# Moving a third of a causal convolution into the stage ahead of it

## The chip, the cores and the metric

The kernel runs on one core of a Trainium2 chip. The metric is the device time of one execution in microseconds (us); the median of 3 runs of the kernel before is 3901.01 us (3900.33 to 3903.65). The engines named below are PE (matrix multiply), DVE (elementwise, the vector engine), ACT (activations, the scalar engine), POOL (elementwise on small things, and one of the queues that issue transfers) and SP (only issues transfers). [...]

## The reference

Two layers on x of shape (4, 512, 128, 64): 4 batches, T = 512 steps, D = 128 x 64 = 8192 columns. The first layer is, for each batch:

```
xn = layernorm(x);  k, v, r = xn @ Wk, xn @ Wv, sigmoid(xn @ Wr)
s_t = decay * s_(t-1) + k_t * v_t            # scan over time
x = x + (r * s) @ Wo
x = x + gelu(conv3 over f of layernorm(x))   # per time step, 64 x 64 channels
xn = layernorm(x)
to = depthwise causal conv over time of xn, 3 taps, + time_b
x = x + layernorm(to) * g + b                # over the 8192 columns of a step
x = x + gelu(x @ W1 + b1) @ W2 + b2          # on the 64 channels
```

The second layer takes a moving average over 25 steps, multiplies the low 128 frequencies of the rest by complex weights, and adds the two. The change touches the first layer only, and there the line `to = ...` and the sums over columns that the layernorm after it needs.

## The kernel before

**Tiling.** In layer 1 the 8192 columns lie on the partitions in 64 chunks of 128, and the 512 time steps lie along the free dimension, so a shift in time is a shift of the free index. Most code handles a pair of chunks at once, a tile of 128 x 2 x 512 (512 KB); a batch has 32 pairs (NPR). Moments over the columns are sums over partitions, and PE makes them by matmuls with a tile of ones.

**Stages of a batch.** J (`project`) makes k, v, r and the statistics of x. Z (`scan`) is the recurrence. A (`attend_and_convolve`) adds the attention, makes the convolution over f, writes the result to DRAM as x2d and sums it. C (`convolve_time`) is the causal convolution: it loads x2d, applies the layernorm with rows rb and mb (one multiply, one subtract), makes three taps, writes the result to DRAM as tod, squares it and sums both. O (`open_feed`) and F (`feed_forward`) load tod and x2d again, make the residual x3 and run the feed-forward, chunk by chunk: `widen` (two matmul groups and two gelus), `narrow` (into the one-bank PSUM tile pa, read by DVE into x4t), `store` (a transpose through PSUM, a copy, a store).

**Order.** The stages are Python generators, and `in_turn` runs two lanes of them against each other: Z, A of batch 0 beside J of 1; C(0) beside A(1); F(0) beside J(2) and Z(2); C(1) beside A(2); F(1) beside J(3) and Z(3); C(2) beside A(3); F(2) beside C(3); F(3) alone. A number in brackets is the batch. `tc.manual_schedule` fixes this written order for PE alone. The orders of DVE, ACT, POOL and of the transfer queues are made by a planner, which places an instruction where its own reckoning finds the engine free, and may draw it far ahead of its place in the source.

**The work of C on one pair** (lines 570 to 586): DVE has the multiply (L570), the subtract into a padded tile xh (L572) and four taps (L579: two for each of the two chunks, each multiplying a shifted view of xh and adding it to `to`); ACT makes the last tap with the bias first (L575) and the squares at the end (L585); POOL zeroes the two columns of padding (L571), adds a correction to the first two time steps (L583) and issues the store (L584); SP issues the load (L547 within `fetch`). PE sums `to` and its squares two pairs later (`add_up`, L249).

**The work of A on one pair**: DVE has three tensor operations of 1024 columns (L482 x1, L486 z, L518 x2). **Of F on two chunks**: DVE has three for the residual (L597, L598, L609) and two x4t (L645); beside it J has two scalings of weights (L355) and two statistics (L342) per pair. J's matmuls are L358; `widen` is L629, `narrow` is L640, the gelus are L633, the transposes L654.

**Buffers.** Tiles with the same tag share a few buffers. C of batches 0 to 2 uses kx (3), kd (2), kh (2, for xh), k3 (3); A uses x1 (3) and z (4), which no stage uses while F stands beside J. The rows rb and mb of C are in the tile rm3, as are those of Z.

Of the kernel before, what the change touches and what calls it, by code (L numbers as in the profile page):

```python
# [10 lines left out]
F32 = mybir.dt.float32  # L11
AF = mybir.ActivationFunctionType
ALU = mybir.AluOpType
# [3 lines left out]
P = 128  # L17
# [5 lines left out]
SL = 512  # L23
NS = D // SL
NPR = NCH // 2
NT = T // P
S = 64
# [14 lines left out]
G1, B1, G2, B2, G3, B3, TB, G4, B4, W0, W1, W2 = range(12)  # L42
# [37 lines left out]
def layer0(ctx, tc, dram, x, xt, vecs, wkvr, wo, wdec, wconv, fbias, w1, fb1, w2, fb2, x4):  # L80
# [4 lines left out]
    nc = tc.nc  # L85
    B = x.shape[0]

    x2d = [dram.tile([NCH, P, T], F32, tag=f"x2_{b}", name=f"x2_{b}") for b in range(B)]
    tod = [dram.tile([NCH, P, T], F32, tag=f"to_{b}", name=f"to_{b}") for b in range(B)]
# [4 lines left out]
    bk = ctx.enter_context(tc.tile_pool(name="bk", bufs=2))  # L94
# [8 lines left out]
    def two(pool, tag):  # L103
        return pool.tile([P, 2, SL], F32, tag=tag, name=tag)
# [16 lines left out]
    def load(name, src):  # L121
        t = const.tile(list(src.shape), F32, name=name)
        nc.scalar.dma_start(t, src)
        return t

    vec = load("vec", vecs)
# [26 lines left out]
    tb_all = const.tile([P, NCH], F32, name="tb_all")  # L153
    fix = const.tile([P, NCH, 2], F32, name="fix")

    halves = [slice(0, H), slice(H, P)]

    def neighbours(q, c):
# [85 lines left out]
    def add_up(st, i, pair, squares, first, last):  # L244

        for j in range(2):
            for k, src in ((0, pair), (1, squares)):
                q = 2 * j + k
                nc.tensor.matmul(  # L249
                    st[32 * q : 32 * q + 32, :], lhsT=ones, rhs=src[:, j, :],  # L250
                    start=first, stop=last,
                )
# [25 lines left out]
    def rows(bank, a, b, names):  # L278
        both = rowp.tile([P, 2, SL], F32, tag=names, name=names)
        for k, col in enumerate((a, b)):  # L280
            pb = bank()
            spread(pb, col)
            nc.scalar.copy(both[:, k, :], pb)
            yield CHAIN
        return both[:, 0, :], both[:, 1, :]

    def pair_of(row):
        return row.unsqueeze(1).to_broadcast([P, 2, SL])
# [6 lines left out]
    def spare(tag, n):  # L295
        return fr.tile([P, 2, n], F32, tag=tag, name=tag, bufs={"z": 4, "wx": 2}.get(tag, 3))

    def c_bank():
        return two(ps_c, "c")
# [9 lines left out]
    carried = {}  # L309
    causal = {}  # L310
    scale = {}
    opened = {}
    begin = {}
    free_s = [True]
    held = [False]
# [53 lines left out]
    def scan(b):  # L369
        kvrg, stt, *left = projected.pop(b)  # L370
        bank = of_p if b == 1 else of_a
        rs, sq = cols("rs1"), cols("sq1")
        mean = cols("mean1")
# [35 lines left out]
            nc.vector.tensor_copy(qo[S:P, 0:S], pq[S:P, 0:S])  # L409
            nc.vector.tensor_scalar_mul(qo[S:P, S:], pq[S:P, S + 2 :], 1.0 / D)  # L410
        gw, bw, qo = sums["gw"], sums["bw"], sums["qo"]
        rb, mb = yield from rows(bank, rs, mean, "rm3")
        if b == 0:
            kv = two(fr, "x1")
        else:
# [42 lines left out]
        rs, mrs = moments(mean2, sq, 2)  # L458
# [84 lines left out]
        carried[b] = moments(mean3, sq3, 3)  # L543

    def fetch(tag, src, b, i):
        t = bk.tile([P, 2, SL + 2], F32, tag=tag, name=tag, bufs=3 if tag == "kx" else 2)[:, :, 0:SL]
        nc.sync.dma_start(t, src[b][2 * i : 2 * i + 2].rearrange("c p t -> p c t"))  # L547
        return t


    def convolve_time(b):
        bank = of_a if b == B - 1 else of_p
        rb, mb = yield from rows(bank, *carried.pop(b), "rm" if b == B - 1 else "rm3")
        st = bank()
        waiting = {}
        for i in range(NPR + 2):
            if i > 1:
                add_up(st, i - 2, *waiting.pop(i - 2), i == 2, i == NPR + 1)
            if i < NPR:
                if b == B - 1:  # L560

                    x2, xr, to = spare("xp", SL), spare("x1", SL), spare("z", SL)
                    xh = spare("wx", 4 * S + SL)[:, :, 0 : SL + 2]
                    sq = two(bk, "sq")
                    nc.sync.dma_start(x2, x2d[b][2 * i : 2 * i + 2].rearrange("c p t -> p c t"))
                else:
                    x2, xr, to = fetch("kx", x2d, b, i), two(bk, "kd"), bk.tile([P, 2, SL], F32, tag="k3", name="to", bufs=3)
                    xh = bk.tile([P, 2, SL + 2], F32, tag="kh", name="xh")
                    sq = bk.tile([P, 2, SL], F32, tag="sq4", name="sq4", bufs=2)
                nc.vector.tensor_tensor(xr, x2, pair_of(rb), ALU.mult)  # L570
                nc.gpsimd.memset(xh[:, :, 0:2], 0.0)  # L571
                nc.vector.tensor_tensor(xh[:, :, 2:], xr, pair_of(mb), ALU.subtract)  # L572
                for j in range(2):
                    c = slice(2 * i + j, 2 * i + j + 1)
                    nc.scalar.activation(  # L575
                        to[:, j, :], xh[:, j, 2:], AF.Identity, bias=tb_all[:, c], scale=vec[:, W2, c]
                    )
                    for k, w in ((1, W1), (0, W0)):
                        nc.vector.scalar_tensor_tensor(  # L579
                            to[:, j, :], xh[:, j, k : SL + k], vec[:, w, c], to[:, j, :], ALU.mult, ALU.add  # L580
                        )
                cc = slice(2 * i, 2 * i + 2)
                nc.gpsimd.tensor_tensor(to[:, :, 0:2], to[:, :, 0:2], fix[:, cc, :], ALU.add)  # L583
                nc.gpsimd.dma_start(tod[b][cc].rearrange("c p t -> p c t"), to)  # L584
                nc.scalar.activation(sq, to, AF.Square)  # L585
                waiting[i] = to, sq
            yield 7.0
        mean, sq = yield from finish(st, bank, 4)
        causal[b] = moments(mean, sq, 4)

# [29 lines left out]
    def feed_forward(b):  # L620
        x3s = opened.pop(b)
        mids, x4s, obs = {}, {}, {}

        def widen(c, m):
            x3 = x3s[c // 2][:, c % 2, :]
            pm = c_bank() if m else two(ps_m, "m")
            for h in range(2):
                hs = slice(h * H, (h + 1) * H)
                nc.tensor.matmul(  # L629
                    pm[:, h, :], lhsT=w1_sb[hs, m * P : (m + 1) * P], rhs=x3[hs, :], start=True, stop=True  # L630
                )
            mid = mids[c, m] = bk.tile([P, 2, SL], F32, tag="mid", name="mid", bufs=4)
            nc.scalar.activation(mid, pm, AF.Gelu_apprx_tanh, bias=fb1_sb[:, m : m + 1])  # L633

        def narrow(c):
            pa = ps_p.tile([P, SL], F32, tag="p", name="pa")
            for m in range(2):
                mid = mids.pop((c, m))
                for h in range(2):
                    nc.tensor.matmul(  # L640
                        pa[h * H : (h + 1) * H, :], lhsT=w2_sb[:, m, :], rhs=mid[:, h, :],
                        start=(m == 0), stop=(m == 1),
                    )
            x4t = x4s[c] = bk.tile([P, SL], F32, tag="x4t", name="x4t", bufs=3)
            nc.vector.scalar_tensor_tensor(x4t, pa, fb2_sb, x3s[c // 2][:, c % 2, :], ALU.add, ALU.add)  # L645
            if c % 2:
                x3s.pop(c // 2)

        def store(c):
            x4t = x4s.pop(c)  # L650
            pool, tag = (ps_s, "s") if free_s[0] else (ps_p, "p")
            pt = pool.tile([P, NT, P], F32, tag=tag, name="pt")
            for t in range(NT):
                nc.tensor.transpose(pt[:, t, :], x4t[:, t * P : (t + 1) * P], ident)  # L654
            s = c // 4
            if c % 4 == 0:
                obs[s] = bk.tile([P, NT, SL], F32, tag="ob", name="ob")
            o = obs[s][:, :, c % 4 * P : (c % 4 + 1) * P]
            if c // 2 % 2:
                for h in range(2):  # L660
                    nc.scalar.copy(o[:, :, halves[1 - h]], pt[:, :, halves[h]])  # L661
            else:
                nc.scalar.copy(o, pt)
            if c % 4 == 3:
                nc.gpsimd.dma_start(  # L665
                    x4[b][:, s * SL : (s + 1) * SL].rearrange("(t p) d -> p t d", p=P), obs.pop(s)
                )

        for c in range(NCH + 2):
            if c < NCH:  # L670
                widen(c, 0)
                widen(c, 1)
            i = c // 2 + 2
            if i < NPR:
                if c % 2:
                    x3s[i] = add_residual(b, i, *coming)
                else:
                    coming = residual(b, i)
            if 0 < c <= NCH:
                narrow(c - 1)  # L680
            if c > 1:
                store(c - 2)
            yield 4.5
# [360 lines left out]
```

## Time and profile before

| | us |
|---|---|
| median of 3 runs | 3901.01 |
| the profiled execution | 3909.18 |
| its span (first to last instruction) | 3907.4 |
| PE busy | 3679.3 (94%) |
| DVE busy | 2686.3 (69%) |
| ACT busy | 1726.6 (44%) |
| POOL busy | 582.5 (15%) |
| transfers, mean over the span | 231 GB/s |
| L579, the taps of C: 384 instructions | 277.0, 745 ns each |
| L640, `narrow`: idle before it, waiting for DVE's x4t | 48.0 |

Busy time is a share of the whole span, and the stages have different limits, so the shares above say little about a single stage. A line of the groups view names the source line, the engine, the operation, what it writes and reads, the size and the count; then its busy time and the mean of one in ns; then how long the engine stood idle just before such instructions, and what ended that. Matmuls overlap one another, so PE's busy time is the time in which at least one was running. In the stages of the first layer, C(0) beside A(1) lies at about 530 to 820 us of the span, F(0) beside J(2) at 850 to 1237, C(1) beside A(2) at 1240 to 1525, F(1) beside J(3) at 1557 to 1940, C(2) beside A(3) at 1945 to 2230, and F(2) beside C(3) up to about 2510.

### The profile page before, as it was taken

The numbers are of one execution on the slowest core, as the hardware profiler recorded it, in microseconds if no ns is written. First come the engines' busy times: TensorE is split into PE (matmuls) and PEld (weight loads), VectorE is DVE, ScalarE is ACT, GpSimd is POOL, SyncE is SP. The second block draws the span as 40 slices with busy tenths as digits, with TensorE's granted clock in tenths as the row PEclk, the third lists the DMA queues.
The fourth block names the chain that finished last, engine by engine and source line by source line (L and its number), as shares of the span: only waits on it lengthen the run. The fifth ranks groups of instructions, "written<-read, shape, count | busy, mean of one in ns | idle before, by whom it ended". The sixth has DMA issues, their size and how long they took to land. (4 is left out here: it accounts for less than half of the span.)

```text
span 3907.4 us, 44936 instructions
## 1 busy us (share of the span) xinstructions
PE 3679.3 (94%) x15945; PEld 1344.5 (34%) x15945; DVE 2686.3 (69%) x3498; ACT 1726.6 (44%) x2427; POOL 582.5 (15%) x1038
## 2 busy tenths in 40 slices
PE   9999998899999898999998888999989999999999
PEld 4433322233333222333322222333322753326533
DVE  4445659975555997555599899955558267892587
ACT  0023345555555564555655588867742210022100
POOL 0000012210000222000022221100014100151011
PEclk9999999999999999999999999999999999999999
DMA  9857647776663777666477677645558468994587
GB/s 310 267 202 250 220 152 250 255 252 237 231 231 142 248 262 253 220 236 235 155 240 244 243 252 256 227 149 185 182 182 286 153 208 295 312 302 149 193 295 268
DMA packets 426166, 901.27 MB, mean 231 GB/s; under 512 B 35864, under 2 KB 86232, under 8 KB 421848
## 3 DMA queue, kind: packets, MB, share of 16 engines
q1 hardware_dynamic: 343552, 621.97, 48.1%
q0 software_dynamic: 79872, 274.77, 19.5%
q8 instruction: 127, 2.08, 0.2%
q10 hardware_dynamic: 2520, 1.67, 0.1%
q14 instruction: 95, 0.78, 0.1%
HBM read 629.77 MB, written 268.50 MB: 230 GB/s over the span
## 5 line engine op out<-in xcount | busy, mean ns | idle before, releaser
L640 PE MATMUL pa<-mid,w_sb 128*64 128x512 f32 x2048 | 498.1, 607 | 48.0 <-DVE x4t L645 48.0
L633 ACT ACTIVATE mid<-m,fb_sb 128x1024 f32<-128x1024 f32 x256 | 284.9, 1113 | 291.1 <-PE m L629 290.7
L645 DVE SCALAR_TENSOR_TENSOR x4t<-pa,fb_sb,x 128x512 f32<-128x512 f32 x252 | 188.0, 746 | 241.2 <-PE pa L640 241.1
L629 PE MATMUL m<-x,w_sb 64*128 64x512 f32 x1008 | 288.3, 644 | 1.5 <-ACT mid L633 0.8
L579 DVE SCALAR_TENSOR_TENSOR to<-xh,vec,to 128x512 f32<-128x512 f32 x384 | 277.0, 745 | 10.7 <-issue 6.8
L633 ACT ACTIVATE mid<-c,fb_sb 128x1024 f32<-128x1024 f32 x256 | 283.3, 1107 | 1.2 <-PE c L629 1.2
L629 PE MATMUL c<-x,w_sb 64*128 64x512 f32 x1008 | 262.7, 594 | 1.3 <-ACT mid L633 1.3
L640 PEld LDWEIGHTS pa<-mid,w_sb 128*64 128x64 f32 x2048 | 124.9, 136 | 391.5 <-issue 229.5
L358 PE MATMUL a<-xp,wx 128*128 128x512 f32 x512 | 241.0, 597 | 6.4 <-DVE wx L355 5.9
L249 PE MATMUL st<-x,ones 128*32 128x512 f32 x512 | 206.4, 616 | 34.3 <-DVE x L518 34.2
L912 PE MATMUL b<-xin,avg_sb 128*128 128x512 f32 x512 | 230.8, 593 | 3.3 <-DVE xin L918 3.3
L918 DVE TENSOR_TENSOR xin<-b,pm 128x512 f32<-128x512 f32 x256 | 159.0, 683 | 97.7 <-PE b L915 82.7
L889 ACT COPY two<-a 128x512 f32<-128x512 f32 x64 | 37.5, 585 | 426.7 <-PE a L884 426.7
L355 DVE TENSOR_SCALAR wx<-wx,vec 128x192 f32<-128x192 f32 x174 | 48.3, 317 | 241.2 <-DMA wx<-in_wkvr 217.4
L665 POOL DMA_DIRECT2D x<-ob x64 | 49.0, 766 | 1049.8 <-ACT ob L661 980.6
L606 ACT ACTIVATE kd<-kd,vec 128x512 f32<-128x512 f32 x256 | 193.6, 809 | 4.3 <-DVE kd L598 4.3
L521 ACT ACTIVATE sq<-x 128x1024 f32<-128x1024 f32 x128 | 134.6, 1051 | 134.7 <-DVE x L518 134.4
L815 DVE TENSOR_TENSOR uv<-xin 128x1024 f32<-128x1024 f32 x128 | 155.8, 1224 | 50.7 <-PE a L829 33.5
L480 PE MATMUL a<-rst,wo_sb 64*128 64x512 f32 x512 | 153.3, 673 | 34.4 <-DVE x L482 33.3
L585 ACT ACTIVATE sq<-to 128x1024 f32<-128x1024 f32 x96 | 101.3, 1055 | 188.7 <-POOL xh L571 183.1
L575 ACT ACTIVATE to<-xh,tb_all,vec 128x512 f32<-128x512 f32 x192 | 149.4, 803 | 77.4 <-DVE xh L572 64.0
L794 DVE COPY xf<-b 128x256 f32<-128x256 f32 x128 | 54.4, 425 | 183.4 <-PE b L858 182.8
(236 smaller groups left out, 6768.2 us busy)
## 6 DMA issues: line engine op xcount, KB each, us to landing
xp<-in_xt SPq DMA_DIRECT2D x256, 512.0 KB
xin<-x SPq DMA_DIRECT2D x128, 1024.0 KB
kx<-x SPq DMA_DIRECT2D x224, 512.0 KB
x<-x POOLq DMA_DIRECT2D x128, 512.0 KB, 4.6
kh<-to SPq DMA_DIRECT2D x128, 512.0 KB
x<-ob POOLq DMA_DIRECT2D x64, 1024.0 KB, 6.6
out<-xin POOLq DMA_DIRECT2D x64, 1024.0 KB, 6.9
to<-to POOLq DMA_DIRECT2D x96, 512.0 KB, 4.2
```

What stands on the lines that cost most here:

```text
L249: nc.tensor.matmul(st[32 * q : 32 * q + 32, :], lhsT=ones, rhs=src[:, j, :], start=first, stop=last,)
L358: nc.tensor.matmul(pa[:, k, :], lhsT=wq[:, j, k * P : (k + 1) * P], rhs=xp[:, j, :], start=first and j == 0, stop=last and j == 1,)
L480: nc.tensor.matmul(at[:, j, :], lhsT=wo_sb[js, :], rhs=rst[js, :], start=True, stop=True)
L579: nc.vector.scalar_tensor_tensor(to[:, j, :], xh[:, j, k : SL + k], vec[:, w, c], to[:, j, :], ALU.mult, ALU.add)
L606: tc.keep_in_program_order(nc.scalar.activation(d[:, j, :], d[:, j, :], AF.Identity, bias=vec[:, B4, c], scale=vec[:, G4, c]))
L629: nc.tensor.matmul(pm[:, h, :], lhsT=w1_sb[hs, m * P : (m + 1) * P], rhs=x3[hs, :], start=True, stop=True)
L633: nc.scalar.activation(mid, pm, AF.Gelu_apprx_tanh, bias=fb1_sb[:, m : m + 1])
L640: nc.tensor.matmul(pa[h * H : (h + 1) * H, :], lhsT=w2_sb[:, m, :], rhs=mid[:, h, :], start=(m == 0), stop=(m == 1),)
L645: nc.vector.scalar_tensor_tensor(x4t, pa, fb2_sb, x3s[c // 2][:, c % 2, :], ALU.add, ALU.add)
L815: nc.vector.tensor_tensor(t, xin[:, 0:2, :], xin[:, 2:4, :], op)
L912: nc.tensor.matmul(po[j], lhsT=avg_sb[:, j, :], rhs=xin[:, j, :], start=True, stop=False)
L918: nc.vector.tensor_tensor(by_n(xin[:, j, :]), by_n(po[j]), by_c(pm[j % 2][:, j // 2, :]), ALU.add)
```

## The change

Twelve of the 32 pairs of the causal convolution of batches 1 and 2 are made one stage earlier, in F(0) and F(1). A generator `convolve_ahead` makes the rows rb and mb in rm3 in its first two steps, and one pair in each of the next twelve; `feed_forward` takes a step of it at every fourth chunk (c = 3, 7, ... 63, of which the first fourteen have something to do). Such a pair is loaded into x1, normalized in place there, made into a tile z and stored to tod. It is not summed then: `convolve_time` of that batch makes the other 20 pairs and, spread among them, loads the twelve back from tod (into kh), squares them on ACT and sums both, so that the sums over all 32 pairs are made in C as before. The rows are taken over from the stage ahead.

The function `taps` holds what both places do. In it the padded tile xh is gone for all batches: the normalized tile stays in xr, and the taps on earlier steps write the shorter views `to[:, j, 1:]` and `to[:, j, 2:]`, so POOL's zeroing is gone as well. The scans of batches 2 and 3 put their rows into rm, since rm3 stays in use from F to C.

```diff
-        rb, mb = yield from rows(bank, rs, mean, "rm3")
+        rb, mb = yield from rows(bank, rs, mean, "rm" if b > 1 else "rm3")
...
+    def taps(b, i, x2, xr, to, rb, mb):
+
+        nc.sync.dma_start(x2, x2d[b][2 * i : 2 * i + 2].rearrange("c p t -> p c t"))
+        nc.vector.tensor_tensor(xr, x2, pair_of(rb), ALU.mult)
+        nc.vector.tensor_tensor(xr, xr, pair_of(mb), ALU.subtract)
+        for j in range(2):
+            c = slice(2 * i + j, 2 * i + j + 1)
+            nc.scalar.activation(
+                to[:, j, :], xr[:, j, :], AF.Identity, bias=tb_all[:, c], scale=vec[:, W2, c]
+            )
+            for k, w in ((1, W1), (2, W0)):
+                nc.vector.scalar_tensor_tensor(
+                    to[:, j, k:], xr[:, j, : SL - k], vec[:, w, c], to[:, j, k:], ALU.mult, ALU.add
+                )
+        cc = slice(2 * i, 2 * i + 2)
+        nc.gpsimd.tensor_tensor(to[:, :, 0:2], to[:, :, 0:2], fix[:, cc, :], ALU.add)
+        nc.gpsimd.dma_start(tod[b][cc].rearrange("c p t -> p c t"), to)
+
+    def convolve_ahead(b):
+
+
+        rb, mb = yield from rows(of_p, *carried[b], "rm3")
+        ahead[b] = rb, mb
+        for i in range(AHEAD):
+            xr = spare("x1", SL)
+            taps(b, i, xr, xr, spare("z", SL), rb, mb)
+            yield
...
     def convolve_time(b):
         bank = of_a if b == B - 1 else of_p
-        rb, mb = yield from rows(bank, *carried.pop(b), "rm" if b == B - 1 else "rm3")
+        made = AHEAD if b in ahead else 0
+        moment = carried.pop(b)
+        if made:
+            rb, mb = ahead.pop(b)
+        else:
+            rb, mb = yield from rows(bank, *moment, "rm" if b == B - 1 else "rm3")
         st = bank()
-        waiting = {}
-        for i in range(NPR + 2):
-            if i > 1:
-                add_up(st, i - 2, *waiting.pop(i - 2), i == 2, i == NPR + 1)
-            if i < NPR:
+        waiting, added = [], 0
+        n = NPR - made
+        for k in range(n + 2):
+            while waiting and waiting[0][0] == k - 2:
+                add_up(st, 0, *waiting.pop(0)[1:], added == 0, added == NPR - 1)
+                added += 1
+            if k < n:
...
+                taps(b, made + k, x2, xr, to, rb, mb)
                 nc.scalar.activation(sq, to, AF.Square)
-                waiting[i] = to, sq
-            yield 7.0
+                waiting.append((k, to, sq))
+                i = k * made // n
+                if i != (k + 1) * made // n:
+
+                    to = fetch("kh", tod, b, i)
+                    sq = bk.tile([P, 2, SL], F32, tag="mid", name="sq5", bufs=4)
+                    nc.scalar.activation(sq, to, AF.Square)
+                    waiting.append((k, to, sq))
+            yield 7.0 * (NPR + 2) / (n + 2)
...
+        early = None
         for c in range(NCH + 2):
+            if b + 2 < B and c % 4 == 3:
+                early = early or convolve_ahead(b + 1)
+                next(early, None)
             if c < NCH:
                 widen(c, 0)
                 widen(c, 1)
```

AHEAD is 12.

More of the change, by code (lines that the diff above doesn't have):

```diff
@@ L154, in layer0 @@
     fix = const.tile([P, NCH, 2], F32, name="fix")
+    AHEAD = 12
     halves = [slice(0, H), slice(H, P)]
@@ L312, in layer0 @@
     opened = {}
+    ahead = {}
     begin = {}
@@ L545, in fetch @@
     def fetch(tag, src, b, i):
-        t = bk.tile([P, 2, SL + 2], F32, tag=tag, name=tag, bufs=3 if tag == "kx" else 2)[:, :, 0:SL]
+        t = bk.tile([P, 2, SL], F32, tag=tag, name=tag, bufs=3 if tag == "kx" else 2)
         nc.sync.dma_start(t, src[b][2 * i : 2 * i + 2].rearrange("c p t -> p c t"))
         return t
+    def taps(b, i, x2, xr, to, rb, mb):
[14 more added lines that the diff above has]
+        nc.gpsimd.dma_start(tod[b][cc].rearrange("c p t -> p c t"), to)
@@ L560, in convolve_time @@
                 if b == B - 1:
[L562 to L565, printed above, removed]
-                else:
-                    x2, xr, to = fetch("kx", x2d, b, i), two(bk, "kd"), bk.tile([P, 2, SL], F32, tag="k3", name="to", bufs=3)
-                    xh = bk.tile([P, 2, SL + 2], F32, tag="kh", name="xh")
+                    x2, xr, to, sq = spare("xp", SL), spare("x1", SL), spare("z", SL), two(bk, "sq")
+                else:
+                    x2 = bk.tile([P, 2, SL], F32, tag="kx", name="x2", bufs=3)
+                    xr, to = two(bk, "kd"), bk.tile([P, 2, SL], F32, tag="k3", name="to", bufs=3)
@@ L569, in convolve_time @@
                     sq = bk.tile([P, 2, SL], F32, tag="sq4", name="sq4", bufs=2)
[L570 to L581, printed above, removed]
@@ L582, in convolve_time @@
-                cc = slice(2 * i, 2 * i + 2)
-                nc.gpsimd.tensor_tensor(to[:, :, 0:2], to[:, :, 0:2], fix[:, cc, :], ALU.add)
-                nc.gpsimd.dma_start(tod[b][cc].rearrange("c p t -> p c t"), to)
-                nc.scalar.activation(sq, to, AF.Square)
-                waiting[i] = to, sq
-            yield 7.0
+                taps(b, made + k, x2, xr, to, rb, mb)
+                nc.scalar.activation(sq, to, AF.Square)
+                waiting.append((k, to, sq))
+                i = k * made // n
```

## The prediction

> **What bounds the kernel now.** I read the page's slices first, then a table by stretch, then the groups and waits inside it. The slices show DVE at 9 in the stretches where one batch's causal convolution (C) stands beside the next one's attention (A), and at 5 where a feed-forward (F) stands beside a projection (J).
>
> ```profile
> PE   9999998899999898999998888999989999999999
> DVE  4445659975555997555599899955558267892587
> ...
> DMA  9857647776663777666477677645558468994587
> ```
>
> Three stretches: A beside J, C(1) beside A(2), F(0) beside J(2). Columns are length, then busy time and count of PE, weight loads, DVE, ACT, POOL, the granted clock, the DMA share and GB/s.
>
> ```profile
> 250.00:450.00 200.00, 197.73 (x845) 61.88 (x848) 111.17 (x147) 62.25 (x86) 17.29 (x24) 1.00 0.75 251
> 1250.00:1500.00 250.00, 227.83 (x1130) 54.74 (x1124) 239.59 (x258) 146.13 (x200) 64.82 (x112) 0.98 0.73 244
> 850.00:1200.00 350.00, 343.78 (x1372) 127.17 (x1368) 195.97 (x259) 196.43 (x260) 11.66 (x18) 1.00 0.64 224
> ```
>
> In the middle row DVE has 96% and, from 1300 on, over 98%; in the other two PE has 98% and DVE 56%. So C beside A is DVE's, F beside J is PE's. The groups of the middle stretch price DVE's work:
>
> ```profile
> L579 DVE SCALAR_TENSOR_TENSOR to<-xh,vec,to 128x512 f32<-128x512 f32 x114 | 83.1, 745 | 3.8 <-issue 2.7 <-ACT to L575 0.8
> ...
> L572 DVE TENSOR_TENSOR xh<-kd,rm 128x1024 f32<-128x1024 f32 x30 | 36.6, 1219 | 0.3
> L570 DVE TENSOR_TENSOR kd<-kx,rm 128x1024 f32<-128x1024 f32 x30 | 36.5, 1218 | 0.1
> ```
>
> and of the F stretch:
>
> ```profile
> L645 DVE SCALAR_TENSOR_TENSOR x4t<-pa,fb_sb,x 128x512 f32<-128x512 f32 x57 | 42.6, 747 | 42.3 <-PE pa L640 42.2
> L609 DVE TENSOR_TENSOR x<-kd,kx 128x1024 f32<-128x1024 f32 x29 | 35.4, 1222 | 2.2
> L342 DVE BATCH_NORM_STATS2 stt<-wx 128x6 f32<-128x512 f32 x54 | 34.7, 685 | 24.1 <-DMA wx<-in_x 23.3
> ...
> L355 DVE TENSOR_SCALAR wx<-wx,vec 128x192 f32<-128x192 f32 x53 | 14.6, 317 | 82.9 <-DMA wx<-in_wkvr 82.9
> ```
>
> [...] the taps on 511 and 510 columns are put at the 745 ns of 512. [...] PE looks 91% busy in C beside A, yet L249 takes 82.2 us for 28 pairs there (twice the matmuls of A alone), against 23.4 for 22 in A beside J. [...] the page's highest slice is 312 GB/s.
>
> **The change part by part.** One tap pair is 2 tensor_tensors and 4 taps: 2 x 1.219 + 4 x 0.745 = 5.42 us on DVE, 2 ACT identities (1.6 us), one POOL fix, one 512 KB load on SP, one store on POOL. Twelve pairs of batch 1 go into F(0), twelve of batch 2 into F(1): 65 us of DVE each.
>
> Gain, C(1) and C(2). Now 28 pairs take 250 us (112 of the L480 instructions, four a pair): 8.93 us a pair; by durations DVE needs 3 x 1.22 (A) + 5.42 = 9.08, so instructions overlap by 2%. After: 3.66 + 5.42 x 20/32 = 7.05 by durations. PE needs for A (197.7 - 73.3 of L358)/22 = 5.65 us a pair, plus 23.4/22 = 1.06 for C's sums: 6.7. The bound is then shared. Best 7.0 (either engine unhindered), worst 8.2 (PE's present 227.8/28 = 8.1 proves to be needed). PE must still wait for squares and x2 in order, and heavy pairs (9.08) alternate with light ones (3.66) over one-buffer PSUM tiles, so I take 7.5: (8.93 - 7.5) x 32 = 46 us a stage, bounds 62 and 23.
>
> Loss, F(0) and F(1). The source calls for a pair every fourth chunk c, up to c = 55. But only PE keeps the written order; in the built program the planner draws the twelve pairs forward: in DVE's order they stand between the x4t of c = 5 and of c = 19 (three first multiplies two chunks earlier). Work there: 3.58 us a chunk as now (0.75 + half of 3 x 1.22 + 2 x 0.317 + 2 x 0.685) x 14 = 50, plus 65 - 3.7 = 61: 111.5, less 2% = 109.5 us. PE makes a chunk in 350/57 = 6.14, fourteen in 86. DVE, at 58%, becomes the bound there and PE waits at L640 for x4t, its one-bank pa. DVE may be late by 6.14 - 1.94 (L640 of one chunk) - 0.75 = 3.4 us for nothing. Added stalls: x1 has three buffers, and in two places a load waits on SP for the last tap of a pair that stands only five DVE instructions (4.2 and 4.7 us) ahead of the multiply that wants it; the chain of waits has loads of this size at 3.3 to 7.2 us (2370 to 2480), and SP must issue first, so some 3 us each. Loss 109.5 + 6 - 86 - 3.4 = 26; F(1)'s order differs little, 25. Bounds: 10 (stalls nil, slack of several chunks) and 65 (below).
>
> The loads and stores: 12 MB more beside 2.8 MB per two chunks (78.5 MB over 57 chunks; 14 chunks 20 MB), 32 MB in 112 us or 285 GB/s, under the 312 seen: hidden, but near. SP's x1 loads stand ahead of J's wx loads, which are wanted eight or more DVE instructions later (10 us): hidden. On ACT 19 us go into a stretch at 56%: hidden; POOL's fixes and stores, at 3%: hidden.
>
> Small items. The first taps of what is left of C, no longer waiting for its rows, come forward into F's last five chunks: 24 us of DVE work instead of 11 against about 22 of PE: 2 us lost a stage, and their gain lies in C. The rows' spreads (8 matmuls, 1.1 us each) only move. Reloads: 6 MB more per C stage while 20 loads and stores become fewer: about 60 MB in 240 us, 250 GB/s as now; the squares keep their number. In-place xr without xh: same DVE count, 96 memsets of 0.1 us off a POOL with room; a kd buffer is held longer, but by DVE itself, in order: 0 (-2 to +5), in C(0) and C(3) too. Scan's rows take "rm", idle then: 0.
>
> Sum: -92 + 51 + 4 = -37 us. The profiled execution, 3909.2 (span 3907.4), would be 3872; it stands 8.2 over the median of 3901.0, which gives 3864.
>
> **The rivals.** (1) Better hiding: in C the pair drops to 7.2 (-55 a stage) and F loses 12: -110 + 24 + 4 = -82, or 3819. For it: DVE ran at over 98% in C, so this order couples well; against: the sum of DVE's work in F's fourteen chunks.
> (2) Slower: DVE's overload in F chains with DMA. Loads at 285 GB/s land later; a late multiply holds x4t, this holds PE; J's loads wait on SP behind the x1 waits, and DVE stands at L355, where it already idles 82.9 us for them. At 3.3 us more of such waiting for each of the twelve pairs F loses 26 + 39 = 65 a stage: 130 + 4 - 92 = +42, 3943. It decides from 44 us lost a stage on. For it: the 82.9; against: those waits arise because DVE is early, and shrink when it is late.
> (3) C doesn't shrink: PE's 8.1 is real, held by the chain of gelu, x2, square and sum in order; the pair takes 8.2, gain 23 a stage: -46 + 55 = +9, 3910. For: the waits for squares at L249 (27 us of weight loads); against: they end at DVE's x2 add.
>
> **How the numbers follow.** My forecast 0.48, rival 1 0.17, rival 2 0.17, rival 3 0.18. The likeliest gives 3864; with 0.3 us either way on the pair in C (19 us over two stages) and 8 us on each F (16), added as squares, its own range is 3839 to 3889. The full range goes from 3815, just under rival 1, to 3920, which takes in rival 3 and leaves most of rival 2 out. What a measurement of this kernel can tell from no change is 0.2%, 8 us. Faster: forecast (0.46) and rival 1 (0.17) and a little of rival 3 = 0.64; same 0.11; slower 0.25.
>
> **What would show it.** Table by stretch: in C(1) beside A(2) 7 to 8 us a pair, DVE under 95%; C(0) beside A(1) as before. In F(0), chunks 6 to 19 take 7.5 to 8.5 us with DVE at 95% or more, waits of PE at pa for DVE about 25 us, and 6.1 before and after. Wrong if those chunks stay near 6.2 (rival 1) or pass 10 (rival 2), if the pair in C stays over 8 (rival 3), or if C(0) or C(3) changes by over 5 us.

## The result, and the profile after

The changed kernel takes 3867.4 us (median of 4 runs, 3859.1 to 3871.1) where the kernel before, run beside it, takes 3900.7: a ratio of 0.991, with a 95% interval of 0.9893 to 0.9928. Its profiled execution took 3868.3 us, with a span of 3866.3, against 3909.2 and 3907.4 before. The forecast was 3864.

Line 672 of the changed kernel (L645 before) writes the tile x4t once for every chunk of a feed-forward. I cut both spans at the starts of these instructions in the timeline: F(0) and F(1) from their first x4t to their last, and what lies between. In F(0) it went from 383.1 to 415.0 us, in F(1) from 378.7 to 410.9. Between the last x4t of F(0) and the first of F(1), where C(1) stands beside A(2), it went from 327.0 to 281.5 us, and the same for C(2) beside A(3) from 310.2 to 265.3. F(0) begins 13.4 us earlier. From the first x4t of F(2) to the end the difference is 1.4 us.

The table by stretch, changed kernel: chunks 5 to 20 of F(0) and the middle of C(1) beside A(2). The pairs of the causal convolution lie close together in those fifteen chunks; I call them the bunch. Columns as in the prediction's table (length, then busy time and count of PE, weight loads, DVE, ACT, POOL, then granted clock, DMA share, GB/s).

```profile
875.30:990.50 115.20, 95.18 (x361) 35.27 (x362) 103.33 (x136) 67.49 (x92) 23.45 (x27) 0.97 0.79 275
...
1280.00:1475.00 195.00, 189.04 (x1070) 49.12 (x1068) 177.32 (x179) 122.26 (x168) 43.02 (x61) 1.00 0.79 264
```

and in the kernel before, the same fifteen chunks of F(0) and a stretch of the same length in C(1) beside A(2):

```profile
887.30:977.70 90.40, 87.49 (x345) 32.03 (x346) 50.15 (x68) 49.54 (x66) 2.26 (x3) 1.00 0.65 228
...
1280.00:1475.00 195.00, 175.68 (x884) 41.42 (x880) 191.83 (x207) 115.81 (x158) 51.94 (x91) 0.99 0.76 254
```

The fifteen chunks take 115.2 us and not 90.4. DVE's work there has doubled. In C(1) beside A(2), 106 matmuls of the attention (four a pair) lie in 195 us, where there were 88: 7.36 us a pair instead of 8.86. DVE fell from 98% to 91% there and PE rose from 90% to 97%, so by busy time PE is now the tighter of the two; e4 below bears on that.

What DVE waited for in those fifteen chunks (columns: total us, times, longest):

```profile
DVE stt L344 <- DMA wx<-in_x: 4.1, 4, 2.4
DVE wx L357 <- DMA wx<-in_wkvr: 2.1, 2, 1.3
...
DVE x L556 <- DMA x<-x: 0.9, 1, 0.9
```

with 2.5 us more in two waits for ACT; and PE, from 875 to 990 us:

```profile
PEld pa L667 <- DVE x4t L672: 27.6, 13, 3.8
PE pa L667 <- DVE x4t L672: 16.7, 11, 3.0
```

PE stood at pa for the x4t of the chunk before. (The two lines don't add up: at 902.2 us a weight load had waited 3.83 us and the matmul behind it 3.01, since the matmul before it ran until 899.19. They come to 44.3 us, and PE was without work for 115.2 - 95.2 = 20 us of the stretch, where it was 3 before.) So 17 of the 24.8 us lost are PE's idle time. In the other 8, PE was busy longer: 16 more of its matmuls lie in the stretch (8 of them spread the rows, which was C's work), and the granted clock was 0.97 instead of 1.00. Over the whole kernel the wait of `narrow` for x4t, the last field of its line on the page, grew from 48.0 us to 73.5, and 22 of these 25.5 lie in the two bunches:

```profile
L667 PE MATMUL pa<-mid,w_sb 128*64 128x512 f32 x2048 | 505.9, 615 | 74.0 <-DVE x4t L672 73.5
```

That these matmuls overlap one another stands in the same line: 2048 of 615 ns are 1260 us by durations, and PE was busy with them for 505.9.

### The profile page after: what moved, and what is told of

The parts are those of the page before. It is cut to its first block, busy times and chain, and to the rows that moved or that the text cites. A ratio compares the mean times of both kernels' runs of the same rounds, so it can differ in the third digit from the quotient of the medians.

```text
span 3866.3 us, 44881 instructions
## 1 busy us (share of the span) xinstructions
PE 3643.1 (94%) x15945; PEld 1343.5 (35%) x15945; DVE 2695.6 (70%) x3498; ACT 1722.6 (45%) x2427; POOL 567.9 (15%) x910
## 5 line engine op out<-in xcount | busy, mean ns | idle before, releaser
L667 PE MATMUL pa<-mid,w_sb 128*64 128x512 f32 x2048 | 505.9, 615 | 74.0 <-DVE x4t L672 73.5
L564 DVE SCALAR_TENSOR_TENSOR to<-kd,vec,to 128x510 f32<-128x510 f32 (+1 forms) x288 | 210.7, 744 | 18.7 <-ACT to L560 16.9
L250 PE MATMUL st<-x,ones 128*32 128x512 f32 x512 | 173.7, 606 | 13.8 <-DVE x L520 13.5
L344 DVE BATCH_NORM_STATS2 stt<-wx 128x6 f32<-128x512 f32 x174 | 113.1, 685 | 101.2 <-DMA wx<-in_x 100.7
L681 PEld LDWEIGHTS pt<-ident,x4t 128*128 128x128 f32 x1024 | 108.3, 141 | 210.9 <-ACT mid L660 155.0
L357 DVE TENSOR_SCALAR wx<-wx,vec 128x192 f32<-128x192 f32 x174 | 48.8, 318 | 189.0 <-DMA wx<-in_wkvr 170.9
```

The source lines that it names most:

```text
L250: nc.tensor.matmul(st[32 * q : 32 * q + 32, :], lhsT=ones, rhs=src[:, j, :], start=first, stop=last,)
L564: nc.vector.scalar_tensor_tensor(to[:, j, k:], xr[:, j, : SL - k], vec[:, w, c], to[:, j, k:], ALU.mult, ALU.add)
L667: nc.tensor.matmul(pa[h * H : (h + 1) * H, :], lhsT=w2_sb[:, m, :], rhs=mid[:, h, :], start=(m == 0), stop=(m == 1),)
```

## The experiments

After the result I held this theory (T1 below): F loses because the planner bunches twelve pairs into fourteen chunks; spread out, they would fit into DVE's spare time. The runs overturned the second half of it. All stretches of the profiled executions, in us, cut at the starts of x4t:

| kernel | F(0) begins | F(0) | its c5 to c20 | its c20 to c40 | C(1) beside A(2) | F(1) | C(2) beside A(3) |
|---|---|---|---|---|---|---|---|
| before | 852.9 | 383.1 | 90.4 | 124.4 | 327.0 | 378.7 | 310.2 |
| before, again (e8) | 846.8 | 383.0 | 90.8 | 124.1 | 327.2 | 380.4 | 314.1 |
| changed | 839.5 | 415.0 | 115.2 | 124.0 | 281.5 | 410.9 | 265.3 |
| changed, again (e10) | 839.8 | 415.1 | 114.8 | 124.0 | 280.4 | 411.3 | 263.2 |
| e1, in-place taps only | 830.2 | 380.6 | 89.9 | 124.2 | 324.7 | 378.7 | 306.7 |
| e2, six pairs | 837.7 | 400.4 | 101.6 | 123.2 | 296.7 | 400.3 | 284.7 |
| e3, every fourth chunk | 840.6 | 450.2 | 113.5 | 150.3 | 278.6 | 405.7 | 263.1 |
| e4, sixteen, every third | 834.7 | 438.3 | 104.2 | 150.4 | 273.2 | 434.2 | 259.9 |
| e5, scalings later | 837.4 | 436.2 | 108.8 | 141.6 | 281.0 | 515.4 | 264.0 |
| e6, one chunk earlier | 840.0 | 424.3 | 98.4 | 135.6 | 284.4 | 409.3 | 263.6 |
| e7, no taps ahead | 839.0 | 408.6 | 109.6 | 123.6 | 279.9 | 408.0 | 263.1 |
| e9, taps first | 838.7 | 383.4 | 89.7 | 121.8 | 280.0 | 393.9 | 263.0 |

Two profiles of the same kernel agree within 2 us on F and within 4 on C; the start of F(0) moves by 6. Line numbers below are those of the changed kernel.

**e1: the in-place taps alone.**

```diff
-            if b + 2 < B and c % 4 == 3:
+            if False and c % 4 == 3:
```

with the scans' rows back in rm3.

> Only the in-place taps of the change are kept: no tap pair is made in F(0) or F(1), no reload, no wider C steps. The whole computation is done. T1 (the gain is DVE work moved out of C; the in-place form is worth about nothing): 3890 to 3900 us, that is 0 to -10 against before; F(0) chunks 5 to 20 take about 90 us as before and C(1), C(2) beside A about 327 and 310 us from F's last x4t to the next F's first. Rival Ra (the 13 us that the changed kernel was already ahead when F(0) began show a gain of the in-place form in every C stage): about 3870 us, with C(1) and C(2) some 10 to 15 us shorter each.

Measured: 0.9967 of the time before (0.9956 to 0.9978), that is 13 us (9 to 17), far from Ra's 31. T1's 10 lies inside that interval and its range of times holds the median, 3894.0 us, but that the form is worth about nothing does not hold. C(1) and C(2) gain 2 to 4 us each, not 10 to 15. Most of what the profiles show lies in C(0) beside A(1). From the first to the last pair of A(1), by the starts of its first DVE operation, the two profiles of the kernel before have 270.1 us both, the ten with in-place taps 258.7 to 263.7; sixteen of these pairs, the 9th to the 25th, take 146.6 us in both and 143.1 to 143.2 in the ten. (e1's profiled execution stood 18 us under its median, so its early start of F(0) says little by itself.) Its table by stretch, the kernel before and then e1:

```profile
620.00:780.00 160.00, 143.32 (x724) 34.14 (x722) 156.90 (x172) 95.29 (x131) 45.68 (x75) 0.97 0.76 255
```

```profile
620.00:780.00 160.00, 146.68 (x739) 34.51 (x738) 159.58 (x175) 98.97 (x136) 45.73 (x58) 1.00 0.77 256
```

DVE's idle time of 3.1 us in 160 is gone. Two thirds of it were one wait of A's last DVE operation for a gelu of ACT, and on ACT this gelu came behind a squaring of C that had itself waited 5.1 us. Such waits are ACT's largest in that stretch of the kernel before:

```profile
ACT sq L585 <- POOL xh L571: 38.8, 18, 5.1
```

The name is that of the zeroing, but the zeroing is not what they waited for. One of them in the timeline of POOL and ACT:

```profile
654.55 0.19 POOL L583 TENSOR_TENSOR to<-to,fix 128x4 f32<-128x4 f32 x1 [4.84 <-issue]
654.68 0.09 POOL L571 MEMSET xh<- 128x4 f32 x1
654.77 1.06 ACT L585 ACTIVATE sq<-to 128x1024 f32<-128x1024 f32 x1 [3.40 <-POOL xh L571]
```

The squares need `to`, and so the last tap and POOL's correction of it (L583). The zeroing of a later pair follows the correction at once and ends 0.03 us after it. It is as close in the other waits (in the one ahead of DVE's, the last tap ended at 724.97, the correction at 727.49 and the zeroing at 727.52), so it accounts for under 1 us of the 38.8. In e1 the squares wait 26.9 us in the same stretch, under other names:

```profile
ACT sq L605 <- DVE to L564: 19.5, 7, 3.2
...
ACT sq L605 <- POOL to L568: 7.4, 3, 2.9
```

and no DVE instruction waits behind them. So e1 shows that the in-place form is worth 9 to 17 us and that DVE's idle time in C(0) went with it. Why it went is open: the planner made other orders of the changed instructions, and the zeroing, the padded tile and the order were not tried apart.

**e2: six pairs instead of twelve.**

```diff
-    AHEAD = 12
+    AHEAD = 6
```

> Six pairs ahead instead of twelve, placed by the planner as in the change (bunched over about six chunks of F). T1 (loss in F is the overload of DVE by the bunch; the gain in C is not linear): F(0) and F(1) lose about 12 us each instead of 25 to 32, C(1) and C(2) gain 28 to 33 each instead of 45: 3850 to 3870 us. Rival Rb (both gain and loss are a price per pair): half of the change's 33 us, about 3884 us.

Measured: 0.9933 (0.991 to 0.9956), or 3875 by the ratio: above T1's 3850 to 3870 and under Rb's 3884, with an interval (3866 to 3884) that reaches both. The bunch itself is as T1 has it: chunks 5 to 20 lose 11.2 us in F(0) and 12.0 in F(1), half of 24.8 and 23.8. But F as a whole loses 17 and 22, since its last five chunks lose 4 to 8 and its first five nearly 2, with six pairs as with twelve; and C gains 30 and 25 (against the kernel before), 4 to 5 us for each pair moved.

**e3 and e4: pairs held to their own places.** The first multiply of a pair is put behind the newest x4t on DVE, so that the planner can't draw it forward; e4 does it with sixteen pairs at every third chunk.

```diff
-                next(early, None)
+                with tc.issue_after(made_x4[0].ins):
+                    next(early, None)
```

> The twelve pairs of the change, but each is held on DVE's order to its own place, behind the x4t of every fourth chunk of F, so that they stand from chunk 10 to chunk 54 and not between 5 and 19. Same instructions. T1 (the bunching costs 25 us a stage): F's chunks 5 to 20 come back to about 95 us, F as a whole loses at most 8 us against before instead of about 32, C(1) and C(2) as in the change: 3815 to 3835 us. Rival Rb (each pair costs about 2 us of F wherever it stands, as the loads, stores and ACT's identities come in PE's way): 3860 to 3870 us, as the change.

> Sixteen pairs ahead, held behind the x4t of every third chunk of F. T1 (DVE has 2.5 us to spare in each chunk of F, and a third-chunk pair of 5.4 us fits): F loses at most 10 us, C's pair goes from about 7.4 to PE's floor near 6.8 to 7.0 us, another 10 to 16 us a stage: 3795 to 3820 us. If PE is already the bound of C beside A with twelve (the rival for this run), no gain over the spread of twelve, or 5 to 15 us worse by what F loses.

Measured: e3 0.9992 (0.998 to 1.0005), e4 0.999 (0.9978 to 1.0003): the whole gain was gone. T1 falls. C kept its gain; F(0) of e3 lost 67 us, more than the 65 us of DVE work that had been put into it, and F(1) only 27. F(0) from chunk 20 to 40 took 150.3 us with five pairs, F(1) 127.3 with five pairs (123.7 before). The same pair costs 5.2 us in one place and under 1 in another, so it isn't the pair's own work (Rb) either. e4's four more pairs shortened C by 5.4 and 3.2 us, about 1 us each, where the first twelve brought 3.8 each, which fits e4's rival: with twelve moved, PE was already busy for 97% of the middle of C(1) (189.0 us of 195).

The rhythm of F(0) shows why. A piece of DVE's timeline in the kernel before (start, duration, line; in brackets the idle time before it and what ended it):

```profile
1002.41 0.75 DVE L645 SCALAR_TENSOR_TENSOR x4t<-pa,fb_sb,x 128x512 f32<-128x512 f32 x1 [1.65 <-PE pa L640]
...
1012.96 0.55 DVE L355 TENSOR_SCALAR wx<-wx,vec 128x192 f32<-128x192 f32 x2 [5.92 <-DMA wx<-in_wkvr]
1013.42 0.74 DVE L645 SCALAR_TENSOR_TENSOR x4t<-pa,fb_sb,x 128x512 f32<-128x512 f32 x1
...
1016.21 0.75 DVE L645 SCALAR_TENSOR_TENSOR x4t<-pa,fb_sb,x 128x512 f32<-128x512 f32 x1 [0.69 <-PE pa L640]
```

and of e3:

```profile
1000.05 0.55 DVE L357 TENSOR_SCALAR wx<-wx,vec 128x192 f32<-128x192 f32 x2 [5.25 <-DMA wx<-in_wkvr]
1000.51 0.75 DVE L673 SCALAR_TENSOR_TENSOR x4t<-pa,fb_sb,x 128x512 f32<-128x512 f32 x1
1001.18 1.22 DVE L556 TENSOR_TENSOR x<-x,rm 128x1024 f32<-128x1024 f32 x1
...
1005.00 2.77 DVE L564 SCALAR_TENSOR_TENSOR z<-x,vec,z 128x511 f32<-128x511 f32 x4 [0.28 <-ACT z L560]
1007.70 0.74 DVE L673 SCALAR_TENSOR_TENSOR x4t<-pa,fb_sb,x 128x512 f32<-128x512 f32 x1
```

In the kernel before, one chunk of 11 us, in which DVE stands 5.9 us at the scaling of J's weights with the x4t behind it, is followed by one of 2.8 in which PE catches up. e3 puts its pair exactly into the short chunk. It becomes 7.2 us, nothing is caught up, and DVE still stands idle for 5 us in front of a scaling. So DVE's 44% of idle time in F isn't room for work anywhere; here it lies before a load.

**e5: the scalings later.** If the scaling in front of the x4t is the trouble, it can go behind it (`x4_done` lists the x4t written so far; the pairs stand as in e3):

```diff
-                nc.vector.tensor_scalar_mul(w, w, vec[:, G1, 2 * i + j : 2 * i + j + 1])
+                with tc.issue_after(x4_done[-1]) if len(x4_done) > 1 and b > 1 else ExitStack():
+                    nc.vector.tensor_scalar_mul(w, w, vec[:, G1, 2 * i + j : 2 * i + j + 1])
```

> As e3 (twelve pairs, each held to its own fourth chunk), and in J(2) and J(3) the two scalings of weights (L357 of the changed kernel) are held on DVE behind the newest x4t, so that in F(0) they stand after an x4t and not right before it. Same instructions. Theory Tc (e3 lost in F because DVE, in order, stood at L357 for the weights' load while the x4t behind it held PE; the weights' load in turn waits for PE to free one of two buffers, so that what a pair delays is never made up): F(0) from chunk 20 to 40 falls from 150 to 125-130 us and the whole F(0) from 450 to below 405, F(1) from 406 to below 400, total 3840 to 3860 us. Rival Tp (a pair standing alone costs its own 5 us whatever stands around it, by DVE's work or by ACT and DMA): F(0) stays at 440 or more, total about 3900 us.

Measured: 1.0237 (1.0207 to 1.0267), slower than everything else. Tc's form of it falls, and neither had F(1) at 515 us. Its waits from 1650 to 1800 us, in F(1):

```profile
PE a L362 <- DVE wx L359: 36.4, 8, 7.1
DVE stt L345 <- DMA wx<-in_x: 31.3, 8, 7.0
```

Now PE waits for the scaled weights, and since its matmuls free the buffers late (four of them end at 1705.27, and SP issues its next loads for J at 1705.30 and 1705.72), the other half of the tile, the statistics' load, comes late as well and holds the x4t in the scaling's stead: DVE waits 6.5 us for it until 1710.26, and the x4t starts at 1711.46. The scaling has a deadline, and moving it past that only renames the wait.

**e6: the pair one chunk earlier in F(0).** Here the scaling stays, and the pair goes where DVE is idle, ahead of it.

```diff
-            if b + 2 < B and c % 4 == 3:
+            if b + 2 < B and c % 4 == (2, 3)[b]:
```

> As e3, but in F(0) the pairs are held one chunk earlier: behind the x4t after which DVE stood idle for 4.6 to 6.0 us at L357 in e3 (chunks 8, 12, ... instead of 9, 13, ...). F(1) is as in e3. Theory Tc: the pair of 5.4 us now fills that idle time; F(0) chunk 20 to 40 falls from 150 to 125-135 us, total 3850 to 3870 us. Rival Tp: no change against e3, about 3900 us.

Measured: 0.9915 (0.989 to 0.9941), 3868 by the ratio, no better than the changed kernel; F(0) took 424 instead of 450, against Tp. But chunks 20 to 40 took 135.6, just outside what Tc expected. Its timeline shows what was left:

```profile
975.51 0.75 DVE L673 SCALAR_TENSOR_TENSOR x4t<-pa,fb_sb,x 128x512 f32<-128x512 f32 x1 [2.17 <-PE pa L668]
976.17 1.22 DVE L556 TENSOR_TENSOR x<-x,rm 128x1024 f32<-128x1024 f32 x1
...
983.88 0.32 DVE L357 TENSOR_SCALAR wx<-wx,vec 128x192 f32<-128x192 f32 x1 [3.08 <-DMA wx<-in_wkvr]
...
985.25 2.73 DVE L564 SCALAR_TENSOR_TENSOR z<-x,vec,z 128x511 f32<-128x511 f32 x4
987.89 0.74 DVE L673 SCALAR_TENSOR_TENSOR x4t<-pa,fb_sb,x 128x512 f32<-128x512 f32 x1
```

The pair's two tensor_tensors lie in the idle time, but a scaling stands between them and the taps. DVE waits 3.1 us for its load, and then the taps, 2.7 us, hold the x4t.

**e7: the bunch without its taps.** The four taps of each pair ahead are left out of the changed kernel.

```diff
-            for k, w in ((1, W1), (2, W0)):
+            for k, w in ((1, W1), (2, W0)) if full else ():
```

> The changed kernel (pairs bunched by the planner) with the four DVE taps of each of the twelve pairs ahead left out, so those pairs hold only the last tap and the bias; loads, the two tensor_tensors, ACT's identities, the fix and the store stay. The planner then puts the twelve pairs between the x4t of c=5 and c=12. T1 (the loss in the bunch is DVE's work: 12 x 2.44 us more in seven chunks, 54 us against PE's 43): the stretch from c=5 to c=20 takes 96 to 101 us, 5 to 11 over before, where the changed kernel took 115. Rival (loads, stores and ACT's share make the loss, and come faster here): 115 us or more.

Measured, one run: chunks 5 to 20 took 109.6 us in F(0), between the two expectations, with 36 us less of DVE's work. From 875 to 945 us DVE waited

```profile
DVE x L556 <- DMA x<-x: 13.0, 4, 4.8
```

where the changed kernel waited 0.9 us for the pairs' loads. So DVE's work set the pace of the bunch, but with that work taken out only 5.6 of the 24.8 us come back. PE's idle time in the stretch fell from 20 us to 13; its busy time, 97 us, did not fall, at a granted clock of 0.94. Behind DVE's work stands a second limit, the loads of the pairs: SP could not issue them for 24 us from 875 to 945, since the three x1 buffers were still being read. Transfers ran at 305 GB/s from 875 to 940, and the number of buffers and the loads' own time were not tried apart.

**e8 and e10: the two kernels again.**

> The kernel before once more, for a second profile. If the 13 us by which the changed kernel was ahead at the start of F(0) come from the in-place taps in C(0), F(0) begins at about 853 us again, and sixteen pairs of A(1) beside C(0) (from its 9th to its 25th) take about 147 us as in the first profile, where the four changed kernels that have been profiled so far took 142. If they come from differences between executions, F(0) begins anywhere from 830 to 853 us.

> The changed kernel once more, timed together with e9, for a direct comparison and a second profile of the bunch in F. T1: F(0) and F(1) from chunk 5 to 20 take 113 to 119 us again, DVE waits there for J's weights and not for the x1 loads, and F(0) begins at 835 to 845 us; time 3860 to 3872 us.

e8 began F(0) at 846.8 us, with 146.6 us for the sixteen pairs as in the first profile. The sixteen pairs alone make 3.4 us of the 13, and from A(1)'s first pair to the start of F(0) there are 329.6 us in both profiles of the kernel before and 324.8 and 322.6 in the two of the changed one: 5 to 7 us belong to the change, and the rest is how late A(1) began. e10 took 0.9913 of the time before (0.9899 to 0.9927) and repeats the bunch: 114.8 and 117.7 us, with 1.1 us of waits at the pairs' loads.

**e9: taps ahead of the scaling.** The scalings that e6 had between multiplies and taps are held behind the last tap; those of every other pair of weights stay where they were. In F(1) the first two pairs stand as in F(0), the others as in e3.

```diff
-                nc.vector.tensor_scalar_mul(w, w, vec[:, G1, 2 * i + j : 2 * i + j + 1])
+                with tc.issue_after(last_tap[0]) if b > 1 and i % 2 == 1 and last_tap[0] is not None else ExitStack():
+                    nc.vector.tensor_scalar_mul(w, w, vec[:, G1, 2 * i + j : 2 * i + j + 1])
...
-            if b + 2 < B and c % 4 == (2, 3)[b]:
+            if b + 2 < B and c % 4 == (2 if b == 0 or c < 16 else 3):
```

> As e6, and the scalings L357 of the pair of weights that stood between the ahead pair's multiplies and its taps in e6 are held on DVE behind the last tap (and so behind the x4t too), while the scalings of every other pair of weights stay where they were; in F(1) the first two pairs stand as in F(0), the other ten behind the x4t of every fourth chunk as in e3. Theory Tc (idle time of DVE at L357 hides a pair only if the whole pair stands ahead of that wait): F(0) from chunk 20 to 40 falls from e6's 136 to 124-130 us and F(0) as a whole from 424 to 395-412, total 3835 to 3860 us. Rival (holding L357 back makes J's matmuls wait for it, as in e5): F(0) at 430 or more, total over 3880 us.

Measured: 3814.1 us, 0.9778 of the time before (0.9764 to 0.9792), and better than Tc expected. F(0) takes 383.4 us with twelve pairs in it, the 383.1 of the kernel before; F(1) 393.9. A stretch of its timeline:

```profile
1014.36 0.75 DVE L675 SCALAR_TENSOR_TENSOR x4t<-pa,fb_sb,x 128x512 f32<-128x512 f32 x1 [1.83 <-PE pa L670]
1015.03 1.22 DVE L558 TENSOR_TENSOR x<-x,rm 128x1024 f32<-128x1024 f32 x1
1016.16 1.22 DVE L638 TENSOR_TENSOR x<-kd,kx 128x1024 f32<-128x1024 f32 x1
1017.29 1.22 DVE L559 TENSOR_TENSOR x<-x,rm 128x1024 f32<-128x1024 f32 x1
1018.43 1.22 DVE L626 TENSOR_TENSOR kd<-kh,rm 128x1024 f32<-128x1024 f32 x1
1019.68 1.22 DVE L627 TENSOR_TENSOR kd<-kd,rm 128x1024 f32<-128x1024 f32 x1
1020.82 2.73 DVE L566 SCALAR_TENSOR_TENSOR z<-x,vec,z 128x511 f32<-128x511 f32 x4
1023.47 0.74 DVE L675 SCALAR_TENSOR_TENSOR x4t<-pa,fb_sb,x 128x512 f32<-128x512 f32 x1
...
1025.32 0.53 DVE L359 TENSOR_SCALAR wx<-wx,vec 128x192 f32<-128x192 f32 x2
1026.54 0.75 DVE L675 SCALAR_TENSOR_TENSOR x4t<-pa,fb_sb,x 128x512 f32<-128x512 f32 x1 [0.69 <-PE pa L670]
```

The whole pair lies between two x4t that were 9.7 to 11 us apart anyway; the scaling comes after the second and no longer waits. The chunks now run 9.1, 3.1, 7.7, 4.5. By the table by stretch, chunks 20 to 40 of F(0) in e9:

```profile
965.63:1087.45 121.82, 121.82 (x481) 44.86 (x482) 91.92 (x120) 74.09 (x101) 10.66 (x15) 1.00 0.81 280
```

and in e3, with as many of DVE's instructions but one:

```profile
990.39:1140.70 150.31, 127.98 (x481) 45.29 (x482) 93.13 (x121) 74.13 (x100) 10.63 (x15) 0.97 0.65 227
```

In e9 PE is busy all the time and DVE 75% of it. The same 481 matmuls kept PE busy for 128.0 us in e3, at a granted clock of 0.97, and for 121.8 in e9, at 1.00: of the 28.5 us between the two, 22 are PE's idle time and 6 are slower matmuls. This version beats both kernels.

## Why the prediction was right, and where it was not

The forecast and its parts, in the order of its steps:

- **C's gain** (46 us a stage, 7.5 us a pair): 45.5 and 44.9, 7.36 a pair over the middle of C(1). By e1, 2 to 4 us of each are the in-place form's and not the moved pairs'. DVE at 91% and PE at 97% fit a shared bound; e4's four pairs at about 1 us each say that most of what was to be had is had. Rival 3 is out.
- **F's loss** (26 and 25 in the fourteen chunks 6 to 19): 27.3 and 24.4 there, from the x4t of c = 5 to that of c = 19, which took 112.4 us instead of 85.1 in F(0); 24.8 and 23.8 from 5 to 20. The working holds in its main term: DVE's durations in these fourteen chunks add up to 112.5 us, and the sum was 111.5. The taps on 511 and 510 columns, put at the 745 ns of 512 as an estimate, took 745 and 742. Two corrections were off and cancelled, which is luck. Instructions overlapped by 9.8 us (112.5 against a busy time of 102.7), 9% and not 2%. The 2% compared durations with the length of a stretch that held idle time as well; the 239.59 us of busy time for 28 pairs in the prediction's own line are 8.56 a pair against 9.08, or 6%. The added stalls came to 10 us and not 6, and not where they were put: 0.9 at the x1 loads, 6.2 at J's loads. DVE was at 90% over the fifteen chunks and not at 95%, and PE was without work for 20 us, where waits of about 25 had been named. Rival 2's mechanism, J's waits growing with DVE's lateness, didn't come: DVE's waits for J's weights in these chunks shrank from 23.7 us to 2.1, as a DVE that is late no longer waits. Transfers did land later: the feed-forward's 1 MB stores (three in each stretch) took a median of 10.1 us from issue to landing in the bunch, at 275 GB/s, and 6.7 in the same chunks of the kernel before, at 228. For the loads it was not shown.
- **F's last chunks** ("2 us lost a stage"): F lost 5.7 and 7.0 after chunk 20, nearly all in the last five chunks, and 1.4 each in the first five, about 15 us in two stages where 4 had been put. e2 shows the same with six pairs, and e1 shows none. That fits C being drawn forward into F once its rows are made ahead, which was not tried by itself.
- **The in-place form** ("0 (-2 to +5), in C(0) and C(3) too"): this step failed. e1 puts the form at 13 us in all (9 to 17). C(0) changed by more than the 5 us that were named as a sign of error: A(1) beside it, from its first pair to its last, went from 270.1 us to 262.5 and 260.3. The working looked at busy time, "a POOL with room", and at one buffer, and not at the 3.8 us that DVE stood idle over sixteen pairs of C(0), which are gone. What removed them is open (see e1). C(3) changed by 2.3, inside the bounds.
- **The sum**: F's ends lost 11 us more than was put, and ahead of F(0) the changed kernel gained 7 to 13 us (against the two profiles of the kernel before) that were not put at all. These two cancel roughly, so that the forecast's 3864 lies closer to 3867 than its parts to theirs; that, too, is luck.

A step behind the sum, that "DVE may be late by 6.14 - 1.94 - 0.75 = 3.4 us for nothing" in a chunk, reads an average as if every chunk had it. In the bunch it didn't matter, since DVE was late throughout. In e3 it is what decides: a chunk of 2.8 us has nothing to spare and one of 11 has 6. The prediction took the loss in F for a matter of how much work stands there; e3, e6 and e9 show, with the same work, 67, 41 and 0 us lost in F(0), by where the pairs and the scalings stand.

Open: how the 15 us that F(1) still loses in e9 divide. 7 of them lie in its last five chunks (32.0 against 24.8), and it was not tried to hold C back from them.

## What to carry to other kernels

Idle time of an engine is a place, not an amount: look in the timeline for what ends it, and put moved work as a whole ahead of that wait, not behind it and not around it. Where a scheduler draws work forward, compare its placing with one held by hand; here a kernel with the same instructions in the same stages took 3814, 3867 or 3901 us. And a side effect that is priced at nothing because its engine is idle deserves a run of its own; when its waits are then read, the name in a wait need not be that of the instruction that took the time: here 38.8 us stood under POOL's zeroing, which ended 0.03 us after the correction and accounts for under 1.

## What the runs showed of the hardware that was not expected

DVE overlapped consecutive instructions: in e9's timeline above, tensor_tensors of 1.22 us start 1.13 us apart where the second doesn't read what the first wrote (1015.03, 1016.16, 1017.29), and 1.25 where one reads what the one before wrote (1018.43, 1019.68). Over the bunch in F(0) this made 9% of the durations' sum (112.5 us against 102.7 busy). And in chunks 20 to 40 of e9's F(0) transfers ran at 280 GB/s, a share of 0.81, beside a PE that was busy for all of the 121.8 us; the kernel before moved 232 GB/s in the same chunks and took 124.4.

The granted clock was 1.00 over chunks 20 to 40 of F(0) in the kernel before, with 2.3 us of PE's idle time, and 0.97 in e3, with 22.3. It did not follow the idle time alone: over the bunch it was 0.97 with 20.0 us idle of 115.2 in F(0) of the changed kernel, and 0.93 with 16.6 of 117.6 in F(1). What lowers it was not tried.
